# A pairwise-product kernel with pairs laid out by right field, the projection read from PSUM, slots of 124 pairs and growing first stores

## The chip, the cores and the metric

The kernel runs on one core of a Trainium2 chip. The metric is the device time in microseconds (us) of one launch. Executions of one kernel mostly agree within 0.1%, so differences of a few us can be read if both kernels run side by side on the same chip. A profiled execution gives a span that is some 2 us shorter than the time; the span runs from the first to the last instruction.

## The reference

For 4096 samples with 32 fields of 64 numbers, every field is projected by a 64 x 64 matrix, and each pair of fields i < j gives the product of the left field with the projected right field.

```python
# x: (4096, 32, 64), W: (64, 64), all float32
vid = jnp.einsum('bfd,de->bfe', x, W)
idx_i, idx_j = jnp.triu_indices(32, k=1)     # 496 pairs
return x[:, idx_i, :] * vid[:, idx_j, :]     # (4096, 496, 64)
```

The output is 520 MB, the input 34 MB. Nearly all the work is writing the output.

## The kernel before

In this kernel TensorE multiplies matrices (512 instructions) and writes its results to PSUM; ScalarE copies them from there to SBUF (64 copies); VectorE forms the products (581 instructions); SyncE issues the stores (104). The host lays x out as 16 tiles of [128 partitions, 32 fields, 128]: two halves of 64 embedding rows, 128 samples along the free axis. The output of a tile is [128, 496 pairs, 128]. One pair is 128 x 128 x 4 B = 64 KB. The parts that matter:

```python
SLOT = 83                      # pairs in one output buffer; 6 stores a tile
xpool: bufs=2   vpool (vid): bufs=2   opool (out): bufs=3   psum: bufs=4

def project(t, order):
    vid = vpool.tile([P, F, C], F32, ...)
    for g in order:                               # groups of 8 fields
        pv = psum.tile([P, GRP, C], F32, ...)
        ...  # 2 x 2 matmuls of 64x64 by 64x512
        nc.scalar.copy(vid[:, g * GRP : (g + 1) * GRP, :], pv)

def products(t, vid, ot, base, a, b, backwards=False):
    ...  # one left field i with a run of right fields j
    nc.vector.tensor_tensor(ot[:, s - base : e - base, :],
        xs[t][:, i : i + 1, :].to_broadcast([P, e - s, C]),
        vid[:, j : j + e - s, :], ALU.mult)

# tile 0 goes backwards, in stores of 10, 18, 27, 26, 42, 41, ... pairs
...
for n, base in enumerate(bases):                  # other tiles
    ot = opool.tile([P, SLOT, C], F32, ...)
    products(t, vid, ot, base, base, top)
    store(t, ot, base, base, top)                 # issued by SyncE
    if 1 <= n <= PIECES and ...:                  # PIECES = 4
        load(t + 1, (n - 1) * F // PIECES, n * F // PIECES, nc.scalar)
```

A store of 83 pairs moves 42,496 contiguous bytes of each partition. It runs on 16 DMA engines, 8 packets (8 partitions) on each, and each engine ends with a 4-byte completion packet: the trace has 128 packets of 42,496 B and 16 completions for such a store, and 1,760 packets of 4 B for the 104 stores and 6 loads on that queue. The stores have SyncE's queue, the later loads ScalarE's; both run on the same 16 engines. VectorE has to wait for a store to land on all 16 before it may fill that slot again: its 86 waits for a store ended 0.09 to 0.47 us after the last of the 16 completions, and the first of the 16 lay 1.2 to 6.2 us before that.

Of the kernel before, what the change touches and what calls it, by code (L numbers as in the profile page):

```python
# [1 line left out]

# [4 lines left out]

F32 = mybir.dt.float32
ALU = mybir.AluOpType

P = 128

C = 128


@with_exitstack
def pairwise_bilinear_kernel(
    ctx: ExitStack,
    tc: tile.TileContext,
    x: bass.AP,  # L20
    w: bass.AP,
    out: bass.AP,
):

    nc = tc.nc
    NT, _, F, _ = x.shape
    D = P // 2
    NP = F * (F - 1) // 2

    GRP = 8  # L30
    NGRP = F // GRP
    BANK = 512 // C

    SLOT = 83
    AHEAD = 2
    PIECES = 4

    off = [i * (F - 1) - i * (i - 1) // 2 for i in range(F)]


    ctx.enter_context(tc.manual_schedule(engines={mybir.EngineType.SP}))

    const = ctx.enter_context(tc.tile_pool(name="const", bufs=1))
    xpool = ctx.enter_context(tc.tile_pool(name="x", bufs=AHEAD))
    vpool = ctx.enter_context(tc.tile_pool(name="vid", bufs=2))
    opool = ctx.enter_context(tc.tile_pool(name="out", bufs=3))
    psum = ctx.enter_context(
        tc.tile_pool(name="ps", bufs=4, space=bass.MemoryType.PSUM)
    )


    w2 = const.tile([P, D], F32)
    nc.scalar.dma_start(out=w2[0:D, :], in_=w)
    nc.scalar.dma_start(out=w2[D : 2 * D, :], in_=w)

    xs = {}

    def load(t, lo, hi, queue=nc.sync):
        if t not in xs:
            xs[t] = xpool.tile([P, F, C], F32, tag="x", name=f"x_{t}")  # L60
        queue.dma_start(out=xs[t][:, lo:hi, :], in_=x[t][:, lo:hi, :])

    def project(t, order):

        vid = vpool.tile([P, F, C], F32, tag="vid", name=f"vid_{t}")
        for g in order:
            pv = psum.tile([P, GRP, C], F32, tag="pv", name=f"pv_{t}_{g}")
            for b in range(0, GRP, BANK):
                f = g * GRP + b
                for h in range(2):  # L70
                    half = slice(h * D, (h + 1) * D)
                    nc.tensor.matmul(  # L72
                        pv[half, b : b + BANK, :],
                        lhsT=w2[half, :],
                        rhs=xs[t][half, f : f + BANK, :],
                        start=True,
                        stop=True,
                    )
            nc.scalar.copy(vid[:, g * GRP : (g + 1) * GRP, :], pv)  # L79
        return vid  # L80

    def products(t, vid, ot, base, a, b, backwards=False):

        fields = [i for i in range(F - 1) if off[i] < b and off[i + 1] > a]
        for i in reversed(fields) if backwards else fields:
            s, e = max(a, off[i]), min(b, off[i + 1])
            j = i + 1 + s - off[i]
            nc.vector.tensor_tensor(  # L88
                ot[:, s - base : e - base, :],
                xs[t][:, i : i + 1, :].to_broadcast([P, e - s, C]),  # L90
                vid[:, j : j + e - s, :],
                ALU.mult,
            )

    def store(t, ot, base, a, b):
        nc.sync.dma_start(out=out[t][:, a:b, :], in_=ot[:, a - base : b - base, :])


    for g in reversed(range(NGRP)):
        load(0, g * GRP, (g + 1) * GRP)  # L100
    load(1, F // 2, F)
    load(1, 0, F // 2)

    for t in range(NT):
        vid = project(t, reversed(range(NGRP)) if t == 0 else range(NGRP))
        bases = list(range(0, NP, SLOT))
        if t == 0:

            ends = [NP, off[27], off[24], off[21], bases[-1]]
            for n, base in enumerate(reversed(bases)):  # L110
                top = min(base + SLOT, NP)
                if n:
                    ends = [top, (base + top) // 2, base]
                ot = opool.tile([P, SLOT, C], F32, tag="o", name=f"o_{t}_{n}")
                for b, a in zip(ends, ends[1:]):
                    products(t, vid, ot, base, a, b, backwards=True)
                    store(t, ot, base, a, b)
        else:
            for n, base in enumerate(bases):
                top = min(base + SLOT, NP)  # L120
                ot = opool.tile([P, SLOT, C], F32, tag="o", name=f"o_{t}_{n}")
                products(t, vid, ot, base, base, top)
                store(t, ot, base, base, top)
                if 1 <= n <= PIECES and t + 1 < NT and t + 1 not in (0, 1):
                    load(t + 1, (n - 1) * F // PIECES, n * F // PIECES, nc.scalar)


_INS = ["r_x", "L0_rec_W"]
_OUTS = [((4096, 496, 64), "float32")]


# [28 lines left out]
```

## Time and profile before

| what | value |
|---|---|
| time | 1298.11 us (1298.02 to 1298.69, 3 runs) |
| span of the profiled run | 1295.9 us |
| bytes moved | 553.82 MB, 427 GB/s over the span |
| VectorE busy | 1105.9 us, 85% |
| TensorE busy | 219.4 us, 17% |
| ScalarE busy | 66.1 us, 5% |

The lines themselves stand in the prediction below. Read them with one question: is the DMA system ever without work? A DMA share near 1.00 in a window means that it is not, and there an idle compute engine costs nothing that is seen (from 113 to 300 us VectorE idles 24 us, at a share of 1.00 and 433 GB/s).

### The profile page before, as it was taken

How to read it: one execution, taken by the hardware profiler on the slowest of the kernel's cores; microseconds unless marked ns; L12 is line 12 of the kernel's file. 1: busy time of each engine (PE TensorE's matmuls, PEld its weight loads, DVE VectorE, ACT ScalarE, POOL GpSimd, SP SyncE). 2: the span in 40 equal slices, each digit the busy share in tenths (PEclk: the TensorE clock that was granted, in tenths of full speed). 3: DMA queues.
4: the chain of work that ended last, by engine and by line, in shares of the span. 5: the costliest groups of instructions: out<-in, count | busy, mean ns of one | idle time of the engine just before them, and what ended most of it. 6: DMA issues, size and time to landing. Idle time of an engine off the chain costs nothing.

```text
span 1295.9 us, 2185 instructions
## 1 busy us (share of the span) xinstructions
PE 219.4 (17%) x512; PEld 55.2 (4%) x512; DVE 1105.9 (85%) x581; ACT 66.1 (5%) x65; POOL 0.2 (0%) x4
## 2 busy tenths in 40 slices
PE   5013022120221302113031120211203122021000
PEld 2000000000000000000000000000000000000000
DVE  6999988889888888888888888888888888888991
ACT  2001000000000000000000000000000000000000
POOL 0000000000000000000000000000000000000000
PEclk9556556565665556655566555655556555565555
DMA  8999999999999999999999999999999999999998
GB/s 337 430 403 442 433 434 432 430 434 431 431 435 435 431 432 434 433 430 435 432 432 436 432 429 432 433 431 431 434 428 431 439 427 438 430 423 444 430 430 353
DMA packets 24077, 553.82 MB, mean 427 GB/s; under 512 B 2817, under 2 KB 2817, under 8 KB 10625
## 3 DMA queue, kind: packets, MB, share of 16 engines
q1 hardware_dynamic: 15840, 524.30, 93.9%
q10 hardware_dynamic: 8224, 29.40, 5.6%
q8 instruction: 4, 0.07, 0.0%
q14 instruction: 9, 0.07, 0.0%
HBM read 33.59 MB, written 520.09 MB: 427 GB/s over the span
## 4 chain that ended last, share of the span: by engine, by line
DMA 63%; DVE 33%; issue 1%; PE 0%; DVEq 0%; ACT 0%
DMA out_dram<-o 63%; DVE o L88 33%; DMA w<-in_L_rec_W_dram 0%; PE pv L72 0%; DVEq L154 0%; ACT vid L79 0%; DVEq L88 0%
## 5 line engine op out<-in xcount | busy, mean ns | idle before, releaser
L88 DVE TENSOR_TENSOR o<-x,vid 128x1408 f32<-128x1408 f32 (+15 forms) x581 | 1105.9, 1974 | 163.7 <-DMA out_dram<-o 152.9
L72 PE MATMUL pv<-x,w 64*64 64x512 f32 x512 | 219.4, 1002 | 958.4 <-DMA x<-in_r_x_dram 953.1
L79 ACT COPY vid<-pv 128x1024 f32<-128x1024 f32 x64 | 64.8, 1012 | 1110.8 <-PE pv L72 1072.2
L72 PEld LDWEIGHTS pv<-x,w 64*64 64x64 f32 x512 | 55.2, 205 | 1120.9 <-issue 1109.1
L79 ACT ACT_TABLE_LOAD x1 | 1.3, 1283 | 2.0 <-issue 2.0
L139 POOL MEMSET const-bfloat16-1.0<- 128x1 bf16 x1 | 0.1, 101 | 0.0
L139 POOL MEMSET const-uint8-127<- 128x1 uint8 x1 | 0.1, 101 | 0.0
L139 POOL MEMSET const-float32-0.0<- 128x1 f32 x1 | 0.1, 98 | 0.2 <-issue 0.2
L139 POOL MEMSET const-float32-1.0<- 128x1 f32 x1 | 0.1, 98 | 0.0
## 6 DMA issues: line engine op xcount, KB each, us to landing
out_dram<-o SPq DMA_DIRECT2D x75, 5312.0 KB, 28.9
out_dram<-o SPq DMA_DIRECT2D x15, 5184.0 KB, 27.6
x<-in_r_x_dram ACTq DMA_DIRECT2D x56, 512.0 KB, 31.8
out_dram<-o SPq DMA_DIRECT2D x5, 2688.0 KB, 10.2
out_dram<-o SPq DMA_DIRECT2D x5, 2624.0 KB, 10.8
x<-in_r_x_dram SPq DMA_DIRECT2D x4, 512.0 KB, 5.8
x<-in_r_x_dram SPq DMA_DIRECT2D x2, 1024.0 KB, 9.8
out_dram<-o SPq DMA_DIRECT2D x1, 1728.0 KB, 5.5
```

The costliest lines, as they stand in the source:

```text
L72: nc.tensor.matmul(pv[half, b : b + BANK, :], lhsT=w2[half, :], rhs=xs[t][half, f : f + BANK, :], start=True, stop=True,)
L79: nc.scalar.copy(vid[:, g * GRP : (g + 1) * GRP, :], pv)
L88: nc.vector.tensor_tensor(ot[:, s - base : e - base, :], xs[t][:, i : i + 1, :].to_broadcast([P, e - s, C]), vid[:, j : j + e - s, :], ALU ...
L139: nc = _bacc.Bacc("TRN2", target_bir_lowering=False, num_devices=1)
```

## The change

Its intent: drop the PSUM copies, free SBUF for larger slots (fewer packets), start VectorE earlier, and let the first stores grow so that the DMA engines never run dry in the head. The core of the diff:

```diff
+SLOT = 124
+GROWING = [21, 15, 19, 23, 27, 19, 29, 18, 19, 20, 38, 28, 24, 25, 47, 34, 29, 61,
+           55, 69, 66, 58, 77, 47, 93, 31]
-    vpool = ctx.enter_context(tc.tile_pool(name="vid", bufs=2))
-        tc.tile_pool(name="ps", bufs=4, space=bass.MemoryType.PSUM)
+        tc.tile_pool(name="ps", bufs=8, space=bass.MemoryType.PSUM)
-    nc.scalar.dma_start(out=w2[0:D, :], in_=w)
-    nc.scalar.dma_start(out=w2[D : 2 * D, :], in_=w)
+    nc.sync.dma_start(out=w2, in_=w)              # W doubled on the host, first in the queue
+    loaded = [load(0, 4, nc.sync), load(1, 2, nc.sync)]
...
+        if 0 < t < NT - 1:
+            loaded.append(load(t + 1, 4, nc.scalar))   # four pieces at once
+        for b in range(0, F, BANK):                    # one bank: four fields, 2 matmuls
+            pv = psum.tile([P, BANK, C], F32, tag="pv", name=f"pv_{t}_{b}")
...
-            nc.scalar.copy(vid[:, g * GRP : (g + 1) * GRP, :], pv)
...
+        for j in range(1, F):                          # right field j with all i < j
...
+                nc.vector.tensor_tensor(
+                    ot[:, at - base : at - base + n, :],
+                    xt[:, i : i + n, :],
+                    vid[j // BANK][:, j % BANK : j % BANK + 1, :].to_broadcast([P, n, C]),
+                    ALU.mult,
+                )
+                if t * NP + at == until or at in (base + SLOT, NP):
+                    nc.sync.dma_start(out=out[t][:, sent:at, :], in_=ot[:, sent - base : at - base, :])
```

The host puts the pairs back into the reference's order. `dynamic_dma_scratch_size=1024` is set there too, to make room for the slots.

More of the change, by code (lines that the diff above doesn't have):

```diff
@@ L13, with first @@
 C = 128
+SLOT = 124
+GROWING = [
+    21, 15, 19, 23, 27, 19, 29, 18, 19, 20, 38, 28, 24, 25, 47, 34, 29, 61,
+    55, 69, 66, 58, 77, 47, 93, 31,
+]
+def first(j):
+    return j * (j - 1) // 2
 @with_exitstack
@@ L28, in pairwise_bilinear_kernel @@
     NP = F * (F - 1) // 2
-    GRP = 8
-    NGRP = F // GRP
     BANK = 512 // C
-    SLOT = 83
-    AHEAD = 2
-    PIECES = 4
-    off = [i * (F - 1) - i * (i - 1) // 2 for i in range(F)]
     ctx.enter_context(tc.manual_schedule(engines={mybir.EngineType.SP}))
     const = ctx.enter_context(tc.tile_pool(name="const", bufs=1))
-    xpool = ctx.enter_context(tc.tile_pool(name="x", bufs=AHEAD))
-    vpool = ctx.enter_context(tc.tile_pool(name="vid", bufs=2))
+    xpool = ctx.enter_context(tc.tile_pool(name="x", bufs=2))
@@ L46, in pairwise_bilinear_kernel @@
     opool = ctx.enter_context(tc.tile_pool(name="out", bufs=3))
     psum = ctx.enter_context(
-        tc.tile_pool(name="ps", bufs=4, space=bass.MemoryType.PSUM)
+        tc.tile_pool(name="ps", bufs=8, space=bass.MemoryType.PSUM)
     )
     w2 = const.tile([P, D], F32)
-    nc.scalar.dma_start(out=w2[0:D, :], in_=w)
-    nc.scalar.dma_start(out=w2[D : 2 * D, :], in_=w)
-    xs = {}
-    def load(t, lo, hi, queue=nc.sync):
-        if t not in xs:
-            xs[t] = xpool.tile([P, F, C], F32, tag="x", name=f"x_{t}")
-        queue.dma_start(out=xs[t][:, lo:hi, :], in_=x[t][:, lo:hi, :])
@@ L63, in project @@
-    def project(t, order):
-        vid = vpool.tile([P, F, C], F32, tag="vid", name=f"vid_{t}")
-        for g in order:
-            pv = psum.tile([P, GRP, C], F32, tag="pv", name=f"pv_{t}_{g}")
-            for b in range(0, GRP, BANK):
-                f = g * GRP + b
-                for h in range(2):
-                    half = slice(h * D, (h + 1) * D)
-                    nc.tensor.matmul(
-                        pv[half, b : b + BANK, :],
-                        lhsT=w2[half, :],
-                        rhs=xs[t][half, f : f + BANK, :],
-                        start=True,
-                        stop=True,
-                    )
-            nc.scalar.copy(vid[:, g * GRP : (g + 1) * GRP, :], pv)
-        return vid
@@ L82, in products @@
-    def products(t, vid, ot, base, a, b, backwards=False):
-        fields = [i for i in range(F - 1) if off[i] < b and off[i + 1] > a]
-        for i in reversed(fields) if backwards else fields:
-            s, e = max(a, off[i]), min(b, off[i + 1])
-            j = i + 1 + s - off[i]
-            nc.vector.tensor_tensor(
-                ot[:, s - base : e - base, :],
-                xs[t][:, i : i + 1, :].to_broadcast([P, e - s, C]),
-                vid[:, j : j + e - s, :],
-                ALU.mult,
-            )
@@ L95, in store @@
-    def store(t, ot, base, a, b):
-        nc.sync.dma_start(out=out[t][:, a:b, :], in_=ot[:, a - base : b - base, :])
-    for g in reversed(range(NGRP)):
-        load(0, g * GRP, (g + 1) * GRP)
-    load(1, F // 2, F)
-    load(1, 0, F // 2)
-    for t in range(NT):
-        vid = project(t, reversed(range(NGRP)) if t == 0 else range(NGRP))
-        bases = list(range(0, NP, SLOT))
-        if t == 0:
-            ends = [NP, off[27], off[24], off[21], bases[-1]]
-            for n, base in enumerate(reversed(bases)):
-                top = min(base + SLOT, NP)
-                if n:
-                    ends = [top, (base + top) // 2, base]
-                ot = opool.tile([P, SLOT, C], F32, tag="o", name=f"o_{t}_{n}")
-                for b, a in zip(ends, ends[1:]):
-                    products(t, vid, ot, base, a, b, backwards=True)
-                    store(t, ot, base, a, b)
-        else:
-            for n, base in enumerate(bases):
-                top = min(base + SLOT, NP)
-                ot = opool.tile([P, SLOT, C], F32, tag="o", name=f"o_{t}_{n}")
-                products(t, vid, ot, base, base, top)
-                store(t, ot, base, base, top)
-                if 1 <= n <= PIECES and t + 1 < NT and t + 1 not in (0, 1):
-                    load(t + 1, (n - 1) * F // PIECES, n * F // PIECES, nc.scalar)
@@ new lines, in pairwise_bilinear_kernel, with load @@
+    nc.sync.dma_start(out=w2, in_=w)
+    def load(t, pieces, queue):
+        xt = xpool.tile([P, F, C], F32, tag="x", name=f"x_{t}")
+        n = F // pieces
+        for lo in range(0, F, n):
+            queue.dma_start(out=xt[:, lo : lo + n, :], in_=x[t][:, lo : lo + n, :])
+        return xt
+    loaded = [load(0, 4, nc.sync), load(1, 2, nc.sync)]
+    done = 0
+    growing = iter(GROWING)
+    until = next(growing)
+    for t in range(NT):
+        if 0 < t < NT - 1:
+            loaded.append(load(t + 1, 4, nc.scalar))
+        xt = loaded[t]
+        vid = []
+        for b in range(0, F, BANK):
+            pv = psum.tile([P, BANK, C], F32, tag="pv", name=f"pv_{t}_{b}")
+            for h in range(2):
+                half = slice(h * D, (h + 1) * D)
+                nc.tensor.matmul(
+                    pv[half, :, :],
+                    lhsT=w2[half, :],
+                    rhs=xt[half, b : b + BANK, :],
+                    start=True,
+                    stop=True,
+                )
+            vid.append(pv)
+        sent = 0
+        for j in range(1, F):
+            i = 0
+            while i < j:
+                at = first(j) + i
+                base = at - at % SLOT
+                if at == base:
+                    ot = opool.tile([P, SLOT, C], F32, tag="o", name=f"o_{t}_{at}")
+                n = min(j - i, base + SLOT - at)
+                nc.vector.tensor_tensor(
[3 more added lines that the diff above has]
+                    ALU.mult,
+                )
+                i += n
+                at += n
+                if t * NP + at == until or at in (base + SLOT, NP):
+                    nc.sync.dma_start(
+                        out=out[t][:, sent:at, :],
+                        in_=ot[:, sent - base : at - base, :],
+                    )
+                    sent = at
+                    if t * NP + at == until:
+                        until += next(growing, NT * NP)
@@ L137 @@
     from concourse.bass_utils import run_bass_kernel_spmd as _run
-    nc = _bacc.Bacc("TRN2", target_bir_lowering=False, num_devices=1)
+    nc = _bacc.Bacc("TRN2", target_bir_lowering=False, num_devices=1, dynamic_dma_scratch_size=1024)
     x = _np.asarray(inputs["r_x"])
+    w = _np.asarray(inputs["L0_rec_W"])
     B, F, D = x.shape
@@ L144 @@
     x = x.reshape(2, NT, C, F, D).transpose(1, 0, 4, 3, 2).reshape(NT, 2 * D, F, C)
+    w = _np.concatenate([w, w])
     arrays, args = {}, []
-    for name, a in zip(_INS, (x, inputs["L0_rec_W"])):
+    for name, a in zip(_INS, (x, w)):
         a = _np.ascontiguousarray(a)
@@ L158 @@
     got = r.results[0]["out_0_dram"].reshape(NT, 2, D, _OUTS[0][0][1], C)
-    return _np.ascontiguousarray(got.transpose(1, 0, 4, 3, 2)).reshape(_OUTS[0][0])
+    order = [first(j) + i for i in range(F) for j in range(i + 1, F)]
+    got = got.transpose(1, 0, 4, 3, 2)[:, :, :, order]
+    return _np.ascontiguousarray(got).reshape(_OUTS[0][0])
```

## The prediction

> **What bounds the kernel now.** I read the page first (busy shares, the slices, the queues, the chain), then the chain in order of time, then windows, then groups by shape, last the records of single transfers. From the page:
>
> ```profile
> PE 219.4 (17%) x512; PEld 55.2 (4%) x512; DVE 1105.9 (85%) x581; ACT 66.1 (5%) x65; POOL 0.2 (0%) x4
> ...
> GB/s 337 430 403 442 433 434 432 430 434 431 431 435 435 431 432 434 433 430 435 432 432 436 432 429 432 433 431 431 434 428 431 439 427 438 430 423 444 430 430 353
> ...
> q1 hardware_dynamic: 15840, 524.30, 93.9%
> q10 hardware_dynamic: 8224, 29.40, 5.6%
> ...
> DMA 63%; DVE 33%; issue 1%; PE 0%; DVEq 0%; ACT 0%
> ```
>
> No compute engine is full. The transfers run at some 432 GB/s in every slice but the first three and the last, so the bulk is bound by the DMA engines, and only head and tail have anything to give. Queue 1 carries the stores (and the first six loads), queue 10 the later loads. Two equations in cost per packet c and rate r of one of the 16 engines, over 16 x 1295.9 us: 0.939 of it = 15840c + 524.30/r and 0.056 of it = 8224c + 29.40/r give r = 27.1 GB/s and c = 9 ns. The single records agree: the median 4,096 B packet took 159 ns, the 42,496 B one 1,571 ns, hence 27.2 GB/s and 8 ns. One pair is 64 KB, or 0.151 us of all engines. The chain in order of time (start, length, what):
>
> ```profile
> 0.74 4.58 DMA w<-in_L_rec_W_dram
> 5.37 4.45 PE pv L72 x9
> 9.84 1.02 ACT vid L79
> 10.89 13.73 DVE o L88 x15
> ...
> 113.00 0.96 DVE o L88
> 113.98 24.27 DMA out_dram<-o
> 138.34 11.79 DVE o L88 x13
> 150.15 27.54 DMA out_dram<-o
> ```
>
> The head hangs on W, eight matmuls, a copy, then VectorE without a break until 113.98; after that store and VectorE alternate because a slot must come free. Windows (length, busy by engine with counts, PE clock, DMA share, GB/s) say what that head costs:
>
> ```profile
> 12.60:113.00 100.40, 19.56 (x66) 6.52 (x62) 100.40 (x48) 9.11 (x9) 0.00 (x0) 0.60 0.97 408
> 113.00:300.00 187.00, 32.63 (x72) 7.63 (x72) 162.75 (x87) 9.11 (x9) 0.00 (x0) 0.55 1.00 433
> 300.00:1293.00 993.00, 159.94 (x352) 37.23 (x352) 841.00 (x445) 44.53 (x44) 0.00 (x0) 0.54 1.00 431
> ...
> 1290.00:1292.00 2.00, 0.00 (x0) 0.00 (x0) 0.00 (x0) 0.00 (x0) 0.00 (x0) 0.50 0.24 104
> 1292.00:1294.00 2.00, 0.00 (x0) 0.00 (x0) 0.00 (x0) 0.00 (x0) 0.00 (x0) 0.50 0.10 41
> ```
>
> VectorE is busy for all of 12.6 to 113 and the DMA engines idle 3% of it, 3 us. Afterwards the DMA share is 1.00: VectorE's waits are free. The last 4 us are a few late engines: the 16 completions of the last store lie between 1288.55 and 1294.61.
>
> [...] an engine takes its queues in turn, a packet from each. The trace agrees, in the times at which a tile's four loads release the matmuls:
>
> ```profile
> 409.51 3.68 PE L72 MATMUL pv<-x,w 64*64 64x512 f32 x8 [35.03 <-DMA x<-in_r_x_dram]
> 423.15 3.68 PE L72 MATMUL pv<-x,w 64*64 64x512 f32 x8 [9.96 <-DMA x<-in_r_x_dram]
> 436.94 3.68 PE L72 MATMUL pv<-x,w 64*64 64x512 f32 x8 [10.12 <-DMA x<-in_r_x_dram]
> ```
>
> They are 13.7 us apart; a load is 8 packets an engine, and 8 store packets of 1.571 us plus 8 of 0.159 make 13.8. [...] No row of this trace has VectorE reading PSUM[...]. The SBUF side is here:
>
> ```profile
> L88 DVE TENSOR_TENSOR o<-x,vid 128x3968 f32<-128x3968 f32 x16 | 68.6, 4291 | 11.3 <-DMA out_dram<-o 11.3
> L88 DVE TENSOR_TENSOR o<-x,vid 128x128 f32<-128x128 f32 x16 | 4.6, 285 | 10.9 <-ACT vid L79 10.9
> ```
>
> The slope is 4006 ns over 3840 elements, 1.043 ns an element, or 133.5 ns a pair. Successive instructions overlap, so what one more costs comes from the total: 1105.9 less 1,015,808 elements x 1.043 (1059.7) is 46 us over 581, 80 ns each.
>
> **The change part by part.**
>
> *Copies gone, vid in PSUM.* 64 copies (64.8 us of ScalarE) go; only the first, 1.0 us, is on the path. VectorE gets 544 instructions (31 right fields and 3 splits at slot edges, 16 tiles) instead of 581[...]. The 8 banks hold one tile's vid. A bank is refilled once VectorE is done with its four fields; even the last, left at the tile's end, is next read only from pair 378 of the next tile, two fills later: no wait of note.
>
> *W first, banks of four fields.* Now the second W copy lands at 6.72 and eight matmuls must follow. After: one W transfer ahead of x on the same queue; the first x piece decides, about 5.3 (it landed at 5.15 behind nothing). Two matmuls instead of eight (some 1.3 us), no copy: VectorE starts at about 6.7 instead of 10.89.
>
> *Growing stores.* This converts the earlier start into time. Before, the first loads keep the DMA until 13.4, and a packet starts 1.1 us after the store's issue. Stores of 10, 18, 27, 26, 42 pairs were issued at 12.61, 15.22, 19.02, 22.70, 28.57. At 0.151 us a pair plus 0.07 the engines are out of work before the first, second, third and fifth by 0.3, 1.0, 1.0 and 1.5 us: 3.8 us in all. After that each store finds work queued. [...] The 4.2 us of earlier start are not to be added: the engines are busy loading then.
>
> *Slots of 124.* Stores drop from 104 to 82; 22 x 128 data packets and 23 x 16 completion packets (one W transfer goes too) are 3184 packets, x 9 ns / 16 engines = 1.8 us. Bytes stay the same. [...]
>
> *Loads.* The pieces of later tiles are the same 4 KB a partition, but all four are issued when VectorE leaves the tile before. By the one-to-one turn a tile's 32 load packets an engine now accompany exactly its 32 store packets, so a load lasts the whole 80 us tile. Piece k lands about 20(k+1) us after issue; VectorE begins that tile about 80 us after issue, and needs the last piece only from pair 276, some 40 us later. Enough.
>
> *Sum.* 1298.1 - 3.8 - 1.8 = 1292.5 us, 0.4% faster. The tail stays.
>
> **Rivals.** (a) VectorE becomes the bound: PSUM reads or the broadcast cost more than estimated. [...] Against it: ScalarE copies 1,024 elements from PSUM in 1,012 ns with no sign of a slow port[...]. About 2%. (b) Loads starve VectorE: if they got less than every second turn, tile starts would wait; 10 us a tile beyond the slack would be +10%. Against it: the 13.7 us steps. (c) Margins at the head fail (a first x piece at 8 us, say): the idle time is partly back, 1294 to 1296. (d) The late engines: two finish 6 us after the earliest, a lag that grew steadily through the run. If it goes with packets, a third fewer store packets takes off up to 2 us more, 1290.5; if with time or bytes, nothing. (e) Packets of 63,488 B bring slow ones with them or fall into pieces: the 1.8 us are lost, 1294.3.
>
> **Range and chances.** Known work in the DMA engines leaves little room: 553.8 MB at 16 x 27.2 is 1273 us without any packet cost or start, already above the 2% line of 1272, so faster by over 2% is nearly excluded. Rivals (c) and (e) pull up 2 to 4 us, (d) down 2. Predicted 1292.5, range 1290 to 1296; chances 0.01, 0.96, 0.03, the last for (a) and (b).
>
> **What would show it.** Right: VectorE starts near 6.7; DMA share 1.00 and above 420 GB/s from 14 to 40 us; some 20,900 packets in all; [...] chain almost all DMA from about 15 us; last slice near 353 GB/s as before. Wrong: matmuls behind x in the bulk with VectorE behind them, a DMA share below 1.00 after 113, VectorE above 1280, or 16-engine completions spread over more than 6 us at the end.

The sum came to 1298.1 - 3.8 - 1.8 = 1292.5 us: both terms are worked out from the trace of the kernel before.

Estimates made afterwards from that trace, with its 80 ns an instruction, its 133.5 ns a pair and no extra cost for PSUM (which it could not show): VectorE 1059.7 + 544 x 0.080 = 1103 us, 69 us a tile against the 80 us that a tile took, so hidden in the bulk; the first five stores issued at about 10.0, 12.1, 14.8, 18.1 and 21.8 us, while the engines have work until 13.4, 16.6, 19.0, 21.9 and 25.5 (from 13.4, with 0.151 us a pair plus 0.07), so that each finds work queued; 17.3 us to fill a slot. The 1.1 us from a store's issue to its first packet is a rough estimate: for the second, third and fifth store, which found idle engines, the trace has 0.83 to 0.99 us over the 16 engines. That takes 0.2 us off the first of the four gaps.

## The result, and the profile after

| | before | after |
|---|---|---|
| time, same rounds | 1298.07 us (1297.90 to 1298.69, 4 runs) | 1298.41 us (1298.05 to 1298.75, 4 runs) |
| ratio, 95% interval | | 1.0002 (0.9984 to 1.0019) |

A ratio is the mean time of one kernel's fast runs over that of the other's of the same rounds, so it is not quite the ratio of the medians quoted.

The predicted 1292.5 us, and the range from 1290, did not come. From the page of the changed kernel (the lines that answer to those of before):

```profile
GB/s 379 430 426 433 438 432 425 434 434 434 428 432 432 434 432 434 431 434 436 432 434 434 426 434 432 430 432 432 432 433 431 434 432 434 432 431 443 425 431 288
...
q1 hardware_dynamic: 12816, 524.33, 93.8%
q10 hardware_dynamic: 8064, 29.36, 5.5%
...
DMA 61%; DVE 34%; issue 1%; DVEq 0%; PE 0%; SPq 0%
```

The packets (single pieces of a transfer, as the trace records them) went down as planned (q1 from 15,840 to 12,816), and the first three slices rose from 337, 430, 403 to 379, 430, 426 GB/s. But the last slice fell from 353 to 288. The gain of the head was given back in the tail. Windows of the changed kernel (length, busy of PE, PEld, DVE and POOL with counts, PE clock, DMA share, GB/s) show both ends:

```profile
12.60:113.00 100.40, 22.39 (x60) 4.75 (x56) 100.40 (x53) 0.00 (x0) 0.54 1.01 430
113.00:300.00 187.00, 33.53 (x74) 7.39 (x76) 175.00 (x87) 0.00 (x0) 0.55 1.01 434
300.00:1293.00 993.00, 163.26 (x360) 37.80 (x356) 818.88 (x401) 0.00 (x0) 0.54 0.99 429
...
1280.00:1290.00 10.00, 0.00 (x0) 0.00 (x0) 0.00 (x0) 0.00 (x0) 0.50 0.48 210
...
1292.00:1294.00 2.00, 0.00 (x0) 0.00 (x0) 0.00 (x0) 0.00 (x0) 0.50 0.15 63
```

In 12.6 to 113 the rate is 430 GB/s where it was 408, with a share of 1.01 where it was 0.97. In 1280 to 1290 the engines are busy only 48% of the time. The same window of the kernel before:

```profile
1280.00:1290.00 10.00, 0.00 (x0) 0.00 (x0) 0.00 (x0) 0.00 (x0) 0.00 (x0) 0.50 0.87 378
```

So most DMA engines finish the changed kernel much earlier, and a few don't. The trace records when each of the 16 engines reports a store as complete. For the last store of some tiles (us from the span's start; "spread" is last less first):

```
            before                              after
tile   first   median    last  spread    first   median    last  spread
  2   256.25   257.10   257.68   1.4    252.30   252.69   254.56   2.3
  4   415.98   416.88   418.67   2.7    412.02   412.40   414.88   2.9
  8   735.76   736.60   739.70   3.9    731.25   731.67   738.52   7.3
 12  1055.64  1057.25  1061.06   5.4   1050.54  1051.48  1061.57  11.0
 15  1288.88  1290.62  1295.08   6.2   1283.29  1284.57  1295.48  12.2
```

(The prediction's 1288.55 to 1294.61 are the ends of the completion packets; these are the same events as they land, some 0.4 us later.) The first engine is 5.6 us ahead of before and the median one 6.05. That is the predicted gain of 5.6. The last engine is 0.4 us behind before. At tile 4 it still led by 3.8 us. It lost that lead tile by tile.

**Which packets are slow.** 6,517 of the 7,168 packets of 63,488 B took exactly 2,342 ns. The time that the others took beyond that adds up to 35.4 us over the 16 engines; this sum over the median is called the excess below. If each slow packet is followed to the one that starts where it ends, until the engine's completion packet, its place in its store is found: of the 208 packets that took over 50 ns more than the median, some 150 are the eighth and last of their store, typically with 2,450 to 2,520 ns. (The trace does not name a packet's engine; 145 to 157 come out, depending on how ties are followed.) They return at most store ends, on the engines that are already behind: of the 157, 127 belong to one of the four engines that finish that store last.

**What else happens then.** This is one engine at a store's end (start us, ns, bytes, queue):

```
608.82  2342  63488  q1     eighth packet of a store
611.16   159   4096  q10    load
611.32     9      4  q1     completion packet: it counts as the store queue's turn
611.32   159   4096  q10    load
611.48  2342  63488  q1     first packet of the next store
```

Of the store queue's 743 completion packets between 260 and 1190 us, 735 start within 10 ns of the end of one load packet and end within 10 ns of the start of another. The completion packet takes the store queue's turn, and an engine has two load packets almost back to back at a store's end (0.16 us from start to start). Engines that are in step (10 or 11 of 16 are within 0.7 us of each other from tile 2 to tile 8) do this together, and an engine that is behind is then in its last store packet. Count the load packets that start on any engine while a store packet (of 42,496 B before, of 63,488 B after) runs:

| load packets starting within a store packet | before: packets, slow (>50 ns) | after: packets, slow |
|---|---|---|
| none | 4449, 2 | 745, 1 |
| 16 or more (one or more per engine in the mean) | 1922, 62 | 2095, 150 |

This is a correlation and not yet a cause. It made the theory for the experiments.

### The profile page after: what moved, and what is told of

It is laid out like the page before. It is cut to its first block, busy times and chain, and to the rows that moved or that the text cites. A ratio compares the mean times of both kernels' runs of the same rounds, so it can differ in the third digit from the quotient of the medians.

```text
span 1296.3 us, 2062 instructions
## 1 busy us (share of the span) xinstructions
PE 225.5 (17%) x512; PEld 52.1 (4%) x512; DVE 1098.1 (85%) x544; POOL 0.2 (0%) x4
## 2 busy tenths in 40 slices
DMA packets 20891, 553.81 MB, mean 427 GB/s; under 512 B 2448, under 2 KB 2448, under 8 KB 10256
## 3 DMA queue, kind: packets, MB, share of 16 engines
q1 hardware_dynamic: 12816, 524.33, 93.8%
## 4 chain that ended last, share of the span: by engine, by line
DMA 61%; DVE 34%; issue 1%; DVEq 0%; PE 0%; SPq 0%
DMA out_dram<-o 61%; DVE o L99 34%; DMA x<-in_r_x_dram 0%; DVEq L145 0%; PE pv L81 0%; DVEq L99 0%; SPq L56 0%
## 5 line engine op out<-in xcount | busy, mean ns | idle before, releaser
L99 DVE TENSOR_TENSOR o<-x,pv 128x2176 f32<-128x2176 f32 (+27 forms) x544 | 1098.1, 2093 | 158.3 <-DMA out_dram<-o 149.5
L81 PE MATMUL pv<-x,w 64*64 64x512 f32 x512 | 225.5, 1025 | 966.3 <-DMA x<-in_r_x_dram 887.2
L81 PEld LDWEIGHTS pv<-x,w 64*64 64x64 f32 x512 | 52.1, 208 | 1138.0 <-issue 1137.4
```

What stands on the lines that cost most here:

```text
L81: nc.tensor.matmul(pv[half, :, :], lhsT=w2[half, :], rhs=xt[half, b : b + BANK, :], start=True, stop=True,)
L99: nc.vector.tensor_tensor(ot[:, at - base : at - base + n, :], xt[:, i : i + n, :], vid[j // BANK][:, j % BANK : j % BANK + 1, :].to_broad ...
```

## The experiments

**Theory A**: loads that take turns with stores slow the stores of engines that are out of step; this makes the late engines. **Rival B**: the larger store packets alone. **Rival C**: some engines are slower per byte, whatever runs; then no schedule helps. "Spread" is always that of the last store's 16 completions in the profiled run.

### Loads on the store queue

```diff
-            loaded.append(load(t + 1, 4, nc.scalar))
+            loaded.append(load(t + 1, 4, nc.sync))
```

> The changed kernel with the later loads issued on the stores' own queue, so that a load no longer takes turns with a store packet by packet. In the changed kernel the last engine of the 16 finished 12.2 us after the first, though the median engine finished 6 us earlier than before. Theory A (loads in turn with the end of a store slow the last packet of a store on engines that are behind): spread at the end under 3 us, 1289 to 1291.5 us. Theory B (the larger store packets of 63,488 B make the spread): spread 12 us, 1297.5 to 1299. Theory C (some engines are slower per byte whatever is done): spread 12 us, 1297.5 to 1299.

Measured: 1296.11 us (1295.03 to 1296.87; before 1298.23), ratio 0.9981 (0.9968 to 0.9995), spread 5.6 us. C, and B taken alone, fall: the same store packets on the same engines, and the spread halves. But A's number is missed too. The excess of the store packets fell from 35.4 to 8.6 us, and that of the later loads' packets rose from 1.9 to 76.1 us (53.7 without the loads of tile 2). It seems that the cost moved from a few engines' stores to the loads of nearly all: the first engine ended at 1288.57 and not 1283.29.

### Each load in one piece

```diff
-            loaded.append(load(t + 1, 4, nc.scalar))
+            loaded.append(load(t + 1, 1, nc.scalar))
```

> The changed kernel with each later load in one transfer of 16 KB a partition, 8 packets an engine and tile instead of 32, still on its own queue: it lies beside one store in four instead of all. Theory A: spread 3 to 6 us, 1290 to 1293 us. Theories B and C: spread 12 us, 1297.5 to 1299.

Measured: 1308.63 us (1308.33 to 1309.06), ratio 1.0080 (1.0067 to 1.0094), spread 18.1 us. I had counted how many store ends lie beside a load; that is wrong. The packets of 16,384 B do more harm than four times as many of 4,096 B: the store packets' excess is 151.6 us. 458 of the 7,168 took over 50 ns more than the median, where it was 208 with 4,096 B. A store packet in which 16 or more load packets started was slower by 280 ns in the mean, against 12 ns with 4 KB packets, and one with none by 1.4 ns. Loads do slow stores, in a burst and by their size.

### Slots of 83

```diff
-SLOT = 124
+SLOT = 83
```

> The changed kernel with slots of 83 pairs (6 stores a tile), everything else kept: PSUM source, order by right field, growing first stores, four loads at once. Theory B: the spread of before, about 6 us, so 1292 to 1294 us. Theory A: the 32 load packets lie beside four of six stores, as before, so also 6 us and 1292 to 1294. Theory C: 12 us, 1297.5 to 1299. It tells C from the others, and whether the start of the changed kernel is worth its predicted 3.8 us.

Measured: 1301.31 us, ratio 1.0022 (1.0010 to 1.0035), spread 8.9 us. The edit was faulty. The list of growing stores advances only when a product ends exactly at its next entry, and with slots of 83 none ends at pair 124. The growth stopped there, and the window 12.6 to 113 had 408 GB/s again. So the run shows by accident that the head's gain hangs on the growing stores. For the slot size it is void, and was done again below.

### The kernel before with its loads on the store queue

```diff
-                    load(t + 1, (n - 1) * F // PIECES, n * F // PIECES, nc.scalar)
+                    load(t + 1, (n - 1) * F // PIECES, n * F // PIECES, nc.sync)
```

> The kernel before with its later loads issued on the stores' queue and nothing else changed. Its spread at the end was 6.2 us. Theory A: spread under 3 us, 1294 to 1296 us. Theories B and C: no change of the spread, 1297.5 to 1299 us.

Measured: 1415.58 us, ratio 1.0903. Neither theory forecast this. Its waits (who waited for what: us in total, times, longest):

```profile
PE pv L72 <- DMA x<-in_r_x_dram: 1096.1, 56, 100.1
DVE o L88 <- ACT vid L79: 292.7, 15, 20.9
```

A piece is now issued by SyncE, in its order after a store. That kernel needs the whole of vid before a tile's first product, so VectorE waits some 20 us at each tile. The DMA engines run dry (share 0.93 from 300 us on) and all fall in step: the spread at the end is 0.2 us. The run says nothing on the theories, but it shows that the second queue does work here which the first can't: in the kernel before, ScalarE issued a tile's four loads in one go (from 471.09 us on, for instance, within 4.46 us) while stores were queued, and their packets stood between those of the stores. From issue to landing a load took 31.8 us there in the median and 21.0 in this run, so at least part of the delay is a later issue; how long a load stood behind store packets in the one queue is not shown.

### Without the later loads, both kernels

The decisive pair. Their outputs are wrong, which doesn't matter for the times. From tile 2 on the x of tiles 0 and 1 is used again.

```diff
-            loaded.append(load(t + 1, 4, nc.scalar))
+            loaded.append(loaded[t - 1])
```

```diff
-                    load(t + 1, (n - 1) * F // PIECES, n * F // PIECES, nc.scalar)
+                    xs[t + 1] = xs[t - 1]
```

> The changed kernel without the loads of tiles 2 to 15 (tiles 0 and 1 are used again; the result is wrong on purpose). 7168 load packets go, 159 ns less 3.5 ns of overlap each, over 16 engines: 69.7 us less at least. Theory A (loads that take turns with stores slow the stores of engines that are out of step, and so make the late engines): the spread of the 16 completions at the end is under 2.5 us instead of 12.2, and the time falls by about 69.7 + 10, to 1217 to 1221 us. Theory C (some engines are slow per byte whatever runs): spread still 11 to 12 us, 1227 to 1230 us. Theory B (large store packets alone): as C.

> The kernel before without the loads of tiles 2 to 15 (result wrong on purpose), the partner of the run without loads of the changed kernel. Theory A: spread under 2.5 us instead of 6.2, 1222.5 to 1226 us; and the changed kernel without loads is faster than it by what the prediction summed (3.8 us of idle in the head and 1.8 us of packets): 4.5 to 6.5 us. Theory C: spread about 6 us, 1227 to 1229 us, and no difference between the two.

Measured: the changed kernel 1220.97 us (1220.72 to 1221.26), spread 1.75 us; the kernel before 1226.56 us (1226.35 to 1226.70), spread 1.4 us. Both spreads are as A forecast them, and far from C's 11 to 12 and 6 us. The time of the changed kernel lies at the upper end of A's range, 6 us under C's; that of the kernel before lies between the two ranges (0.6 us above A's, 0.4 under C's) and doesn't tell them apart, but C had no difference between the two kernels. The two kernels differ by 5.6 us, just the sum of the prediction (3.8 + 1.8). The windows show the first term where it was expected (16 GB/s more over 100.4 us are 1.6 MB, or by estimate 3.7 us at the bulk's 433 GB/s). Changed kernel without loads, then the kernel before without loads:

```profile
12.60:113.00 100.40, 24.82 (x68) 4.99 (x64) 100.40 (x53) 0.00 (x0) 0.56 1.01 430
```

```profile
12.60:113.00 100.40, 26.80 (x112) 11.82 (x108) 100.40 (x50) 10.85 (x11) 0.00 (x0) 0.63 0.97 414
```

So the gain is real, large store packets alone make no late engines, and the loads take the gain away.

### One piece on the store queue

```diff
-            loaded.append(load(t + 1, 4, nc.scalar))
+            loaded.append(load(t + 1, 1, nc.sync))
```

> The changed kernel with each later load as one transfer of 16 KB a partition on the stores' own queue. On the store queue in 4 KB pieces the load packets themselves were slow (53 us summed over the engines, 3.4 each) and the spread was 5.6 us. Theory A (what counts is reads of some engines beside writes of others, per packet): 24 fewer packets an engine and tile save 16 x 24 x 8 ns = 3 us, and fewer bursts to be out of step with: 1291 to 1294 us. Rival D (what counts is the bytes read beside writes): no gain but the packets, 1294 to 1297 us.

Measured: 1297.76 us, but from 1293.44 to 1304.00 in six runs, ratio 0.9997 (0.9978 to 1.0016); spread 10.9 us in the profiled one. The load packets' excess is 79.4 us (53.4 without the load of tile 2), as with four times as many of a quarter of the size. That speaks for rival D, but with this scatter it is inconclusive.

### Slots of 83, the list mended

```diff
-SLOT = 124
+SLOT = 83
-                if t * NP + at == until or at in (base + SLOT, NP):
+                if t * NP + at >= until or at in (base + SLOT, NP):
-                    if t * NP + at == until:
+                    while t * NP + at >= until:
```

> The changed kernel with slots of 83 pairs and the list of growing first stores mended for it (in the first trial the list stuck at pair 124, so the first stores did not grow and the start's gain was lost; tile 0 landed 5 us later than in the changed kernel). Tile 0 should land near 92 us as in the changed kernel. If slots of 124 are the cause of the larger spread (theory B), spread 6 us and 1293 to 1295 us. If the four loads issued at once, one beside each store, are (theory A), spread about 9 us as in the first trial, and 1296 to 1298 us.

Measured: 1295.66 us (1295.11 to 1296.95; before 1298.32), ratio 0.9982 (0.9970 to 0.9994), spread 4.9 us, first engine at 1287.40. With loads as in the changed kernel, the smaller slot keeps the last engine 3.2 us ahead of the changed kernel's, although 41 more pairs in a slot had saved the first engine 4.1 us. Tile 0 landed at 96 to 98 us instead of 92: the cuts at 83 add small stores. The run keeps PSUM, the pair order and the four loads at once, so these alone do not make the spread of 12 us.

### Slots of 124, stored in halves

```diff
+                    cuts = [sent, (sent + at) // 2, at] if t > 1 else [sent, at]
+                    for a, b in zip(cuts, cuts[1:]):   # one store for each
```

> The changed kernel with each slot of 124 pairs of tiles 2 to 15 stored by two transfers of 62 pairs issued one after the other: the same slots and waits, packets of 31,744 B instead of 63,488. It tells the size of a packet from the size of a slot. 32 more packets an engine and tile cost 14 x 32 x 8 ns = 3.6 us on every engine, so the first engine should end near 1287 instead of 1283.3. If the bytes of a store packet beside a load make the late engines: spread 4 to 6 us, 1294 to 1296 us. If the slot of 124 (buffering, rhythm of VectorE) does: spread 12 us, 1301 to 1303 us.

Measured: 1295.32 us (1295.10 to 1296.70), ratio 0.9980 (0.9967 to 0.9992), spread 6.6 us, first engine at 1287.45. With the slot, buffers and rhythm of VectorE unchanged, only the packets halved, the spread falls to about that of the kernel before. The 3.6 us of extra packets are paid, about as calculated (the first engine is 4.2 us later, the median one 3.8), and still the kernel gains, because the last engine counts. The excess of its store packets is 41.4 us, no less than the 35.4: smaller packets did not remove the slow time.

### Slots of 100, four slots of 83, and loads spread

```diff
-SLOT = 83      # the mended version above
+SLOT = 100
```

> The changed kernel with slots of 100 pairs (5 stores a tile, packets of 51,200 B), growing list mended as in the run with slots of 83. If the spread grows with the size of slot or packet, it lies between the 4.9 us of 83 and the 12.2 us of 124: 7 to 10 us, 1295.5 to 1298 us. If 124 is special because its 32 load packets just fill the tile's 32 store packets, the spread is that of 83, 4 to 6 us, and the time 1293.5 to 1295.5 us.

Measured: 1294.84 us (1294.57 to 1295.21; before 1298.42), ratio 0.9974 (0.9961 to 0.9986), spread 6.4 us, first engine at 1285.44. This has the lowest time of the correct versions, 0.26% faster than the kernel before; against the changed kernel only through their ratios to before (0.9974 and 1.0002). Its lead of 0.8 us on slots of 83 is not shown: the intervals of the two ratios overlap. Its windows:

```profile
300.00:1280.00 980.00, 164.54 (x356) 35.18 (x356) 827.77 (x409) 0.00 (x0) 0.53 1.00 433
1280.00:1290.00 10.00, 0.00 (x0) 0.00 (x0) 0.00 (x0) 0.00 (x0) 0.50 0.61 265
1290.00:1292.00 2.00, 0.00 (x0) 0.00 (x0) 0.00 (x0) 0.00 (x0) 0.50 0.00 0
```

The tail is over before 1292, where the changed kernel still had two engines at work.

```diff
-    opool = ctx.enter_context(tc.tile_pool(name="out", bufs=3))
+    opool = ctx.enter_context(tc.tile_pool(name="out", bufs=4))   # slots of 83
```

> The run with slots of 83 pairs and the mended list, with four slots instead of three (332 pairs of buffer against 372 in the changed kernel and 249 with three). If buffer depth lets the engines drift apart: spread 8 us or more, 1297 us or more. If depth doesn't matter: spread 4 to 6 us, 1294.5 to 1296.5 us, as with three.

Measured: 1296.17 us (1295.76 to 1296.55), ratio 0.9984 (0.9971 to 0.9996), spread 6.8 us, between the two expectations: depth makes at most a small difference.

The next run takes out the four loads at once and puts in, shortened:

```diff
+                    if 0 < t < NT - 1 and at == base + SLOT and 1 <= n <= 4:   # slots of 83
+                        # load piece n - 1 of tile t + 1, on ScalarE's queue
```

> The run with slots of 83 pairs and the mended list, with the loads issued one piece after each of the stores 1 to 4 of a tile, as the kernel before does. If four loads at once matter beside the slot size: spread under 4 us and 1293 to 1295 us; if not, the same 4.9 us and 1295 to 1296.5 us. Three parts of the changed kernel are then left over the kernel before (PSUM source, pair order, first stores), so it should be faster than it by about the idle 3.8 us of the head in either case.

Measured: 1295.89 us (1295.22 to 1296.80), ratio 0.9983 (0.9969 to 0.9996), spread 6.5 us. With slots of 83 it makes no difference that is seen here whether four pieces are issued at once or one after each store; with 124 this was not tried. Over the kernel before there is left a gain of 2.5 us and not 3.8. The run has 26,076 packets where the kernel before has 24,077; at the prediction's 9 ns these 2,000 would cost every engine 1.1 us, an estimate that accounts for most of the difference.

### Slots of 120 and 112, and half the loads

```diff
-SLOT = 83      # the mended version above
+SLOT = 120     # the next run: 112
```

> The changed kernel with slots of 120 pairs and the mended list: packets of 61,440 B, 3% smaller than with 124, but five stores a tile (the last of 16 pairs). If the bytes of a packet make the late engines: spread 10 to 13 us, 1297 to 1300 us. If full cover of the stores by loads does (32 load packets beside 40 store packets here): spread 5 to 8 us, 1294 to 1296.5 us.

Measured: 1310.24 us (1307.03 to 1312.41), ratio 1.0090. The spread is 1.9 us, which neither side expected: here all engines are late, the first one at tile 8 by 7 us against the changed kernel (738.38 and 731.25). The fifth store has 16 pairs and occupies one of the three slots. VectorE's longest wait for a store rose from 5.0 to 10.9 us, and the slow packets' excess is 119 us in large stores, 49 in the small ones and 43 in the loads. This is another loss, and I did not take it apart; for the question asked the run is void.

> The changed kernel with slots of 112 pairs and the mended list: packets of 57,344 B, five stores a tile (the last of 48). By bytes: spread 8 to 11 us, between those of 100 and 124, 1296 to 1298 us. By cover: spread 5 to 7 us as with 100, 1294 to 1295.5 us.

Measured: 1297.67 us, from 1294.94 to 1301.59 in six runs, ratio 0.9995 (0.9982 to 1.0009). The profiled run was the one of 1294.94, with a spread of 6.6 us. The median is where the rule "by bytes" put it, the profiled spread where "by cover" put it: inconclusive.

```diff
-            loaded.append(load(t + 1, 4, nc.scalar))
+            loaded.append(loaded[t - 1])      # wrong on purpose: half of x is stale
+            for lo in (0, 8):
+                nc.scalar.dma_start(out=loaded[t + 1][:, lo : lo + 8, :], in_=x[t + 1][:, lo : lo + 8, :])
```

> The changed kernel, slots of 124, with only the first two of the four loads of tiles 2 to 15 (the other half of x is kept from two tiles before; the result is wrong on purpose): the same store packets, 16 load packets an engine and tile beside 32. Half of the 69.7 us of load packets go. If the loss is in proportion to the store ends that meet a load: spread 6 to 8 us, 1257 to 1260 us. If it needs full cover: spread 2 to 5 us, 1254 to 1257 us. If loads only start the drift and anything keeps it up: spread 10 to 12 us, 1261 to 1264 us.

Measured: 1256.90 us (1256.53 to 1257.36), spread 4.6 us: with the same store packets and half the load packets, the spread falls to well under half. Yet the excess of the store packets is 30.5 us, not much under the 35.4 of all loads. It is spread over more engines (the median engine is 1.9 us behind the first, where it was 1.3). So the sum of the slow packets does not decide (storing in halves says the same), but whether they fall on the engines that are behind: of the 159 slow packets that end a store here, 32 belong to the four engines that finish it last, where it was 127 of 157. That the reduced lag follows from this is a reading, not a test.

## Why the prediction was wrong

The engines' last-tile completions, in one table (us; no-load runs are not comparable in time with the rest):

| run | first | median | last | spread | time |
|---|---|---|---|---|---|
| before | 1288.88 | 1290.62 | 1295.08 | 6.2 | 1298.07 |
| after | 1283.29 | 1284.57 | 1295.48 | 12.2 | 1298.41 |
| after, loads on store queue | 1288.57 | 1290.17 | 1294.20 | 5.6 | 1296.11 |
| after, stored in halves | 1287.45 | 1288.33 | 1294.04 | 6.6 | 1295.32 |
| after, slots of 100 | 1285.44 | 1286.86 | 1291.82 | 6.4 | 1294.84 |
| before, no later loads | 1222.67 | 1222.92 | 1224.10 | 1.4 | 1226.56 |
| after, no later loads | 1216.30 | 1216.65 | 1218.05 | 1.75 | 1220.97 |

**The step that failed** is the last sentence of the sum, "The tail stays", with its support in rival (d): "If it goes with packets, a third fewer store packets takes off up to 2 us more, 1290.5; if with time or bytes, nothing." I had seen the late engines and allowed the spread to shrink or to stay. It doubled, from 6.2 to 12.2 us, and these 6.0 us are the whole of the missing 5.9 (1298.4 less 1292.5). What the runs showed in its place: the spread is not a property of some engines; it is made by the loads (1.75 us without them, 12.2 with them) together with the stores of 124 pairs in one piece (5 to 7 us with packets of 31,744, 42,496 or 51,200 B, the faulty trial of 83 having 8.9; the runs with 57,344 and 61,440 B were inconclusive). The prediction's own signs of being wrong had this one, completions spread over more than 6 us at the end, but set where it told little: the kernel before already had 6.2.

**The copies and PSUM.** Right that it is hidden, wrong in size: the total that is cut from it held an extra cost for PSUM. VectorE was busy 1098.1 us with its 544 instructions; without that cost the estimate is 1103. Two shapes of the changed kernel:

```profile
L99 DVE TENSOR_TENSOR o<-x,pv 128x3968 f32<-128x3968 f32 x16 | 68.5, 4281 | 0.0
...
L99 DVE TENSOR_TENSOR o<-x,pv 128x128 f32<-128x128 f32 x16 | 4.6, 287 | 50.0 <-DMA out_dram<-o 41.7 <-PE pv L81 8.3
```

They were 4291 and 285 ns from SBUF: no extra cost is seen with one operand in PSUM. Rival (a) is out.

**W first, small banks.** The direction was right, the size not. VectorE began at 8.29 us and not 6.7; the kernel before began at 10.89. The chain in order of time has it:

```profile
1.17 4.98 DMA x<-in_r_x_dram
...
6.28 3.57 PE pv L81 x8
```

The first x piece landed at 6.14 us and not 5.3, and the two first matmuls took until 8.29, 2 us and not 1.3. That VectorE began 1.6 us later than predicted cost nothing that is seen: the DMA share from 14 to 40 us was 1.01.

**Growing stores.** Right. The first stores were issued at 12.18, 14.31, 16.97, 20.17 and 23.90 us, some 2.1 us later than the estimate beside the prediction (1.6 of them from VectorE's later start), and the first loads kept the engines until about 14.2 instead of 13.4. From 14 to 40 us the share was 1.01 and the rate 429 GB/s (0.90 and 379 before), with no 2 us window under 395. Rival (c) is out.

**Slots of 124.** The packets came out as counted (20,891 in all). In the chain a slot took VectorE 16.96 to 17.67 us to fill, from 215 us on. Without loads the 1.8 us are in the time (5.6 us less the 3.7 of the head); with them they are on the engines that are not late. Rival (e) came nearest to what happened: the large packets do bring slow ones, but only with loads beside them (208 over 50 ns, and 17 without), and the loss was not 1.8 but 5.9 us.

**Loads.** Right in what it said: two groups of matmuls were released 20.2 us apart.

```profile
602.20 3.67 PE L81 MATMUL pv<-x,w 64*64 64x512 f32 x8 [16.49 <-DMA x<-in_r_x_dram]
622.40 3.68 PE L81 MATMUL pv<-x,w 64*64 64x512 f32 x8 [16.53 <-DMA x<-in_r_x_dram]
```

VectorE did not starve, so rival (b) is out. But I asked only whether the loads arrive in time, not what their turns do to the stores beside them. This change makes a tile's 32 load packets accompany exactly its 32 store packets. The prediction states this as reassurance; the loss came from these loads beside these stores, though the one-to-one lock itself is not shown to be the cause.

**What stays open.** That loads slow stores, and that this together with slots of 124 made the late engines, is shown by runs. Why a burst of loads slows another engine's store (in the memory, or on the way to it) is not. Nor is it settled whether 124 is bad for the bytes of its packets or because its store and load packets are locked one to one, so that the same engines meet the burst at every store's end. Storing in halves and halving the loads are at home in both readings; slots of 112 and 120 were meant to decide and did not. The burst at the store's end is a correlation of the packet records.

## What to carry to other kernels

This DMA-bound kernel ended with its slowest DMA engine (the last completion at 1295.48 us of a span of 1296.3, the median one at 1284.57): look at the spread of the engines' completions over the run, not only at the mean share, before counting a gain in the head or in packets. Here loads ran beside stores, and a change that made the packets larger and locked the two streams together lost in the late engines (spread 12.2 us, 6.2 before) what it had saved in packets and in the head; 83 and 100 pairs a store both beat 124, through their ratios to the kernel before (0.9982 and 0.9974 against 1.0002). To know whether a gain was never there or was taken away, remove the suspect from both kernels and compare the two.
